# Statistics moved to ScalarE, weight loads to GpSimd's queue, and a rounding remainder made by TensorE

## Chip, cores and metric

The kernel runs on one core of a Trainium2 chip. The metric is the device time in microseconds of one execution of the whole kernel. The engines of the core are named as in the profile: PE (TensorE, with PEld for its weight loads), DVE (VectorE), ACT (ScalarE), POOL (GpSimd) and SP (SyncE, which here only issues DMAs).

## What is computed

The input x has 4 images of 16 channels and 256 x 256 pixels, in fp32. Two layers follow, each with a residual and a group normalization in front (8 groups of 2 channels).

```python
# layer 0: a convolution gives 25 logits per channel and pixel; their softmax weighs the 5x5 patch
h = gn(x)
logits = conv3x3(h, conv_w) + conv_b            # N, 16*25, H, W
weights = softmax(logits.reshape(N, C, 25, H, W), axis=2)
x = x + einsum('ncuij,ncuij->ncij', unfold5x5(h), weights)
# layer 1: a 3x3 convolution over silu(h) and over 8 cubic B-splines of h
h = gn(x)
x = x + conv(silu(h), base_w) + conv(bspline(h), spl_w) + bias
```

## The kernel before

**Stages.** The *prologue* (lines 394 to 575) loads x in eight tiles (image and half of the rows; line 413), takes group statistics with VectorE's bn_stats (lines 524 and 526; group_stats, line 133), writes each image's normalizing scale and bias to nrm, prepares the weights of both layers (prepare0, prepare1; the raw weights are loaded by lines 421 to 447), and bounds the logits. It also normalizes image 0. *Layer 0* (layer0, line 603) has two copies in the program, of which a flag selects one; here the one without a maximum runs. *Layer 1* (layer1, line 831) goes over 64 units of 16 rows.

**Normalization.** normalize (line 242) is a generator of small steps. For image b it fills zero borders in DRAM (lines 248 to 259), and for each group of 4 channels applies the scale and bias on ScalarE in two layouts: hsp by rows (line 317, stored to hs) and ht for transposition (line 330). Its inner part columns (line 339), 16 calls per image, has TensorE transpose four blocks into the PSUM tile tp (line 352), copies tp to tt (fp32) and to hi (fp32r, which rounds h), and takes the rest lo = tp - hi on VectorE (line 360). The three are stored to DRAM with line 292. SyncE's queue issues all of these DMAs. For image 0 the steps are pulled along by the prologue's loop over the tiles of x, with tp copied to tt by VectorE; for images 1 to 3 by layer 0 on the image before, one step of the generator per step of layer 0 (line 817), with ScalarE as copier. So 48 calls of columns lie in the first 48 strips of layer 0.

**Layer 0.** The work is cut into 64 strips: image, half of the rows (128 of them on the partitions), and 32 columns of the picture. A strip has 8 steps of 4 columns. For each column, TensorE multiplies the im2col columns am (fp32) and an (fp32r) by the weights, into one of three PSUM buffers lg of two columns each (lines 780 and 784). ScalarE takes Exp of two columns at a time to e (line 803); GpSimd multiplies e by the patch values u (line 808); VectorE sums numerators and denominators to nd (line 685). e has four buffers. am and an come from hst and hsl by SyncE's queue (lines 633 and 643). What follows a strip is put on a list with due steps (after and step, lines 673 to 681): seed (ScalarE, Ln and Exp, lines 698 and 699), divide (VectorE, lines 703 to 705), apply (GpSimd, line 711, which subtracts the quotient from the tile xc of x), and, once four strips have filled an xc of 128 columns, statistics (VectorE's bn_stats, line 719) and store (ScalarE's DMA queue, line 729). statistics feeds the second group normalization: scales (line 171) turns st1 into the factors of layer 1, for images 0 and 1 during the last image of layer 0, for 2 and 3 during layer 1.

**Order.** in_order (line 577) makes every engine keep the program's order in layer 0 and in layer 1; the marks of lines 821 and 823 allow SyncE and ScalarE to begin layer 1's work beside the last strips of layer 0, but the first Silu of layer 1 stays behind ScalarE's last instruction of layer 0 (line 1041). In the prologue the order within an engine isn't fixed by hand.

**Layer 1.** Per unit ScalarE makes the distances and powers (lines 931, 161 to 164) and Silu (line 913), VectorE the splines (lines 156 and 165 to 167), TensorE the products (lines 977 to 993).

```python
            def sums():
                nd, j, e, done = waiting.pop(0)
                nc.vector.tensor_reduce(
                    nd[:, :, j : j + JG, :], e.rearrange("p t j m c d -> p t j c m d"),
                    AX.XY, ALU.add,
                )
```

Of the kernel before, what the change touches and what calls it, by code (L numbers as in the profile page):

```python
# [14 lines left out]
ALU = mybir.AluOpType  # L15
# [18 lines left out]
def conv_preact_kernel(  # L34
# [95 lines left out]
    stat1 = ctx.enter_context(tc.tile_pool(name="stat1", bufs=1))  # L130
    st1 = [const.tile([P, G, NH * (W // CX), 6], F32, name=f"st1_{b}") for b in range(B)]

# [38 lines left out]
    def scales(b, psum):  # L171


        def small(n, name):
            return stat1.tile([P, n], F32, name=f"{name}_{b}", tag=f"{name}{b % 2}")

        mv = stat1.tile([P, G, 2], F32, name=f"mv_{b}", tag=f"mv{b % 2}")
        for g in range(G):
            nc.vector.bn_aggr(mv[:, g, :], st1[b][:, g].rearrange("p n s -> p (n s)"))
        yield  # L180
        ps = psum()[:, 0:G]
        nc.tensor.matmul(ps, lhsT=ones, rhs=mv[:, :, 0], start=True, stop=True)
        yield
        mean, d, rstd = small(G, "mean"), small(G, "d"), small(G, "rstd")
        q = stat1.tile([P, 6], F32, name=f"q_{b}", tag=f"q{b}")
        nc.vector.tensor_sub(d, mv[:, :, 0], ps)
        nc.vector.tensor_mul(mean, gsel_sb, ps)
        nc.vector.reduce_sum(q[:, 1:2], mean, AX.X)
        yield
        nc.scalar.activation(d, d, AF.Square)  # L190
        yield
        ps = psum()[:, 0:G]
        nc.tensor.matmul(ps, lhsT=ones, rhs=d, start=True, stop=False)
        nc.tensor.matmul(ps, lhsT=ones, rhs=mv[:, :, 1], start=False, stop=True)
        yield
        nc.vector.tensor_scalar(rstd, ps, EPS, None, ALU.add)  # L196
        yield
        nc.gpsimd.tensor_tensor(rstd, rstd, mhalf, ALU.pow)  # L198
        nc.gpsimd.tensor_mul(rstd, rstd, gsel_sb)
        yield  # L200
        nc.vector.reduce_sum(q[:, 0:1], rstd, AX.X)
        nc.vector.tensor_scalar(q[:, 1:2], q[:, 1:2], q[:, 0:1], -1.0, ALU.mult, ALU.mult)
        for k in range(2):
            nc.vector.tensor_scalar(q[:, 2 + k : 3 + k], q[:, k : k + 1], 2.5, None, ALU.mult)
        yield
        ps = psum()[:, 0:2]
        nc.tensor.matmul(
            ps, lhsT=sel.rearrange("p c s -> p (c s)"), rhs=q[0:C, 2:4], start=True, stop=True
        )
        yield  # L210
        nc.vector.tensor_copy(q[:, 4:5], ps[:, 0:1])
        nc.vector.tensor_add(q[:, 5:6], ps[:, 1:2], ub)
        sc[b] = tuple(q[:, k : k + 1] for k in (0, 1, 4, 5))
        yield
# [3 lines left out]

    nrm = [const.tile([P, 2, G], F32, name=f"nrm{b}") for b in range(B)]
    NIM = 3  # L220

    def norm_tiles(prep):
# [6 lines left out]
        ]  # L229
        for t in (*tts, *xps):  # L230
            nc.gpsimd.memset(t, 0.0)
        for t in (*his, *los):
            nc.gpsimd.memset(t.bitcast(F32), 0.0)
        return prep, xps, tts, his, los
# [6 lines left out]

    def normalize(b, ptr, tiles, held=None, copier=None):

        prep, xps, tts, his, los = tiles
        copier = copier or nc.scalar.copy
        for e in (0, HP - PAD):
            for r in range(PAD):
                nc.sync.dma_start(  # L250
                    hs[b][:, e + r].rearrange("s c w -> c s w"),
                    zero[0:C, 0 : NST * SP].rearrange("c (s w) -> c s w", s=NST),
                )
        for h in range(NH):
            for w in (0, (W + 1) * RP):
                nc.sync.dma_start(hst[b][h][:, w : w + RP], zero[0:C, 0:RP])
                nc.sync.dma_start(
                    hsl[b][h][:, :, w : w + RP].rearrange("c t r -> (c t) r"), zero[:, 0:RP]
                )
# [79 lines left out]
        def columns(q, n, h):  # L339
# [11 lines left out]
            for k in range(QG):  # L351
                nc.tensor.transpose(
                    tp[:, k, :], hts[q, h][:, n * QG + k].rearrange("p w c -> p (w c)"), ident
                )
            yield
            copy(tts[n], copier)
            copy(his[n], nc.scalar.copy)
            yield

            nc.vector.tensor_sub(  # L360
                los[n][:, h, :, 1 : 1 + P], tp, his[n][:, h, :, 1 : 1 + P].bitcast(F32)
            )
            if h == NH - 1:
                moves.append((5, partial(border, los[n])))
                moves.append((9, partial(put_columns, q, n)))
            yield
            yield
# [26 lines left out]
    with tc.tile_pool(name="prep0", bufs=2) as prep, tc.tile_pool(  # L394
# [42 lines left out]
        for d in range(3):  # L437
            dc = slice(d * C, (d + 1) * C)
            for k in range(9):
                nc.sync.dma_start(sw[:, d, k], spl_w[dc, k])  # L440
            v = spl_s[dc]
            nc.sync.dma_start(
                ss[:, d],
                bass.AP(tensor=v.tensor, offset=v.offset, ap=[v.ap[0], [0, NS], [1, 9 * nm]]),
            )
        bw = pre.tile([nm, 9, nm], F32, name="bw")
        nc.sync.dma_start(bw, base_w)

# [67 lines left out]
        for b in range(B):  # L516
# [27 lines left out]
            nc.vector.tensor_copy(nrm[b][:, 0], rstd)  # L544
            nc.vector.scalar_tensor_tensor(nrm[b][:, 1], mean, -1.0, rstd, ALU.mult, ALU.mult)
            ms = stat.tile([P, 2], F32, name=f"ms_{b}", tag="ms")
            nc.vector.tensor_mul(mean, mean, mean)
# [11 lines left out]
            if b == 0:  # L559
                ahead = normalize(0, ptr0, tiles, held, nc.vector.tensor_copy)  # L560
                next(ahead)
# [41 lines left out]
    def layer0(shift):  # L603
# [4 lines left out]
        with tc.tile_pool(name=f"prep{arm}", bufs=2) as prep, tc.tile_pool(  # L608
# [7 lines left out]
            for t in ans:  # L616
                v = t.bitcast(F32)
                nc.vector.memset(v, 0.0)
                for r in (4 * C, 6 * C):
                    nc.vector.memset(v[r : r + 1], 1.0)  # L620
            tiles = norm_tiles(prep)
# [80 lines left out]
            def divide(n, nd, xc, r):  # L702
                nc.vector.tensor_mul(nd[:, 0], nd[:, 0], r)  # L703
                nc.vector.scalar_tensor_tensor(r, nd[:, 0], 2.0, r, ALU.subtract, ALU.mult)  # L704
                nc.vector.tensor_mul(nd[:, 1], nd[:, 1], r)  # L705
                after(LAG + 3, apply, n, nd, xc)

            def apply(n, nd, xc):
                w0 = strips[n][2] * SW % CX
                v = xc[:, :, w0 : w0 + SW]  # L710
                nc.gpsimd.tensor_sub(v, v, nd[:, 1].rearrange("p j c -> p c j"))  # L711
                if w0 + SW == CX:
                    after(2, statistics, n, xc)

            def statistics(n, xc):
                b, hf, s = strips[n]
                k = hf * (W // CX) + s * SW // CX
                for g in range(G):
                    nc.vector.bn_stats(  # L719
                        st1[b][:, g, k, :],  # L720
                        xc[:, g * GC : (g + 1) * GC, :].rearrange("p c w -> p (c w)"),
                    )
                after(2, store, n, xc)

# [106 lines left out]
    def layer1(arm, last, marks):  # L831
# [3 lines left out]
        with ExitStack() as pools:  # L835
# [135 lines left out]
            def outputs(n, sx):  # L971
# [29 lines left out]
            more = chain(*(  # L1001
                scales(b, lambda: pstat.tile([P, 8], F32, name=f"ps{arm}", tag="ps"))
                for b in range(2, B)
# [92 lines left out]
```

## Time and profile before

| what | value |
|---|---|
| median of three timed runs | 3113.82 us (3112.22 to 3114.83) |
| the profiled execution | 3113.9 us |
| its span in the profile | 3112.0 us, 40438 instructions |
| busy over the span | DVE 3010.4 us, PE 2845.3, ACT 2083.5, POOL 1938.2, PEld 1494.9 |
| granted TensorE clock | 0.965 of full speed, mean |
| prologue, layer 0, layer 1 | to about 144 us, to 2110 us, to the end |

A row of the stretches gives, for each engine, the busy time and the number of instructions in the stretch, then the granted TensorE clock, the mean busy share of the 16 DMA engines and what they moved. A row of the groups gives line, engine, operation, output and inputs, shapes and count, then busy time in us, the mean duration of one in ns, and the idle time of the engine just before, with what ended it. A row of the chain or of the timeline begins with its start and duration in us. SPq is the issue of DMAs by SyncE. The duration of one instruction is some hundredths of a microsecond longer than the distance to the next one's start, since neighbours overlap; sums over a stage are made from starts.

### The profile page before, as it was taken

What the parts mean: (1) busy time and instruction counts of PE and PEld (TensorE: products, weight loads), DVE (VectorE), ACT (ScalarE), POOL (GpSimd) and SP (SyncE); (2) the same over time, 40 slices, a digit from 0 to 9 for tenths busy, and PEclk for the clock granted to TensorE, in tenths of its full rate; (3) what the DMA queues carried; (4) which work ended last, traced back from release to release, by engine and by line L of the source; (5) the groups of instructions that cost most, each with busy time, mean ns of one, the idle gap of its engine ahead of it and who ended that gap; (6) DMA issues with size and microseconds to landing.
All of it is one profiled execution on the core that took longest, in us unless ns stands there. A gap on an engine that the chain in (4) does not pass through costs nothing.

```text
span 3112.0 us, 40438 instructions
## 1 busy us (share of the span) xinstructions
PE 2845.3 (91%) x14776; PEld 1494.9 (48%) x14776; DVE 3010.4 (97%) x1733; ACT 2083.5 (67%) x2107; POOL 1938.2 (62%) x659
## 2 busy tenths in 40 slices
PE   3489999999999999999899999976999999999999
PEld 2356656656565566566565665641232223222222
DVE  6689999999999999999999999999999999999997
ACT  6466655456564465555444444458999999999996
POOL 2289999999999999999999999990000001000000
PEclk7699999999999999999999999998999999999999
DMA  7978878778877778788676666659999889999994
GB/s 222 309 206 232 241 207 224 194 212 223 239 218 214 204 198 234 215 223 231 186 192 168 167 177 180 166 135 199 193 196 195 197 193 192 194 196 197 193 197 92
DMA packets 356530, 626.34 MB, mean 201 GB/s; under 512 B 45298, under 2 KB 222692, under 8 KB 340452
## 3 DMA queue, kind: packets, MB, share of 16 engines
q1 hardware_dynamic: 323300, 606.88, 78.0%
q10 hardware_dynamic: 33024, 16.78, 1.9%
q8 instruction: 121, 1.98, 0.3%
q14 instruction: 85, 0.70, 0.1%
HBM read 513.95 MB, written 104.24 MB: 199 GB/s over the span
## 4 chain that ended last, share of the span: by engine, by line
DVE 69%; PE 11%; ACT 6%; issue 6%; DMA 5%; SPq 2%; POOL 0%; DVEq 0%; ACTq 0%; POOLq 0%
DVE nd L685 48%; PE lg L780 5%; PE yp L977 4%; DVE ta L166 3%; DVE ta L165 3%; DVE tb L166 3%; DVE tb L165 3%; DVE ring L167 2%; DMA xin<-in_x_dram 2%; PE lg L784 1%; DVE st L719 1%; DVE tb L156 1%; DVE r L704 1%; DMA sx<-x1s 1%; DVE nd L703 1%
## 5 line engine op out<-in xcount | busy, mean ns | idle before, releaser
L780 PE MATMUL lg<-wm,am 128*128 128x400 f32 x4096 | 1750.2, 508 | 122.5 <-ACT e L803 108.2
L808 POOL TENSOR_TENSOR e<-e,u 128x1600 f32<-128x1600 f32 x512 | 1788.8, 3536 | 69.4 <-ACT e L803 68.2
L685 DVE TENSOR_REDUCE nd<-e 128x128 f32<-128x3200 f32 x512 | 1747.5, 3476 | 23.3 <-POOL e L808 23.2
L803 ACT ACTIVATE e<-lg 128x800 f32<-128x800 f32 x1024 | 815.8, 836 | 896.6 <-DVE nd L685 762.7
L784 PE MATMUL lg<-wn,an 97*128 97x400 f32 x2048 | 1359.3, 664 | 0.1
L780 PEld LDWEIGHTS lg<-wm,am 128*128 128x128 f32 x4096 | 766.7, 194 | 449.4 <-ACT e L803 159.2
L977 PE MATMUL yp<-ring,wt 128*32 128x512 f32 x6144 | 737.9, 594 | 53.8 <-POOL ring L948 35.5
L784 PEld LDWEIGHTS lg<-wn,an 97*128 97x128 f32 x2048 | 391.1, 191 | 311.9 <-issue 15.7
L977 PEld LDWEIGHTS yp<-ring,wt 128*32 128x32 f32 x6144 | 210.9, 108 | 571.1 <-issue 454.0
L894 POOL MEMSET sx<- 16x256 f32 x8 | 2.4, 302 | 718.5 <-PE yp L985 278.6
L993 PE MATMUL yp<-sl,ws 64*32 64x512 f32 x1536 | 176.5, 588 | 0.0
L167 DVE SCALAR_TENSOR_TENSOR ring<-ta,ta 128x2048 f32<-128x2048 f32 (+1 forms) x64 | 147.9, 2310 | 2.5
L167 DVE SCALAR_TENSOR_TENSOR ring<-tb,tb 128x2048 f32<-128x2048 f32 x64 | 145.7, 2276 | 2.6
L166 DVE TENSOR_TENSOR ta<-ta,ta 128x2048 f32<-128x2048 f32 (+1 forms) x64 | 147.3, 2301 | 0.1
L166 DVE TENSOR_TENSOR tb<-tb,tb 128x2048 f32<-128x2048 f32 x64 | 145.3, 2271 | 0.0
L913 ACT ACTIVATE sl<-sx,q 64x2048 f32<-64x2048 f32 x64 | 133.5, 2085 | 0.3 <-DMA sx<-x1s 0.3
L164 ACT ACTIVATE ta<-ta 128x2048 f32<-128x2048 f32 (+1 forms) x64 | 123.2, 1925 | 2.0
L164 ACT ACTIVATE tb<-tb 128x2048 f32<-128x2048 f32 x64 | 120.5, 1883 | 0.8 <-POOL sx L894 0.6
L711 POOL TENSOR_TENSOR xc<-xc,nd 128x512 f32<-128x512 f32 x64 | 98.8, 1544 | 11.9 <-DVE nd L705 11.9
L198 POOL TENSOR_TENSOR rstd<-rstd,mhalf 128x8 f32<-128x8 f32 x4 | 7.5, 1866 | 158.0 <-DVE rstd L196 158.0
L993 PEld LDWEIGHTS yp<-sl,ws 64*32 64x32 f32 x1536 | 48.8, 106 | 116.2 <-issue 115.9
L931 ACT ACTIVATE xta<-xta,q 128x4096 f32<-128x4096 f32 (+4 forms) x23 | 83.7, 3640 | 0.0
(171 smaller groups left out, 1917.2 us busy)
## 6 DMA issues: line engine op xcount, KB each, us to landing
am<-hst SPq DMA_DIRECT2D x512, 194.6 KB
u<-hs SPq DMA_DIRECT2D x320, 288.0 KB
an<-hsl SPq DMA_DIRECT2D x512, 129.8 KB
xta<-x1s SPq DMA_DIRECT2D x40, 1024.0 KB
xtb<-x1s SPq DMA_DIRECT2D x40, 1024.0 KB
xtc<-x1s SPq DMA_DIRECT2D x40, 1024.0 KB
am<-hst SPq DMA_DIRECT2D x256, 129.8 KB
sx<-x1s SPq DMA_DIRECT2D x248, 128.0 KB
```

What stands on the lines that cost most here:

```text
L164: nc.scalar.activation(s1, r1, AF.Square, scale=2.0)
L165: nc.vector.scalar_tensor_tensor(s2, t, 2.0, s2, ALU.subtract, ALU.mult)
L166: nc.vector.tensor_mul(s1, s1, r1)
L167: nc.vector.scalar_tensor_tensor(f, s2, 0.0, s1, ALU.min, ALU.subtract if given else ALU.add)
L685: nc.vector.tensor_reduce(nd[:, :, j : j + JG, :], e.rearrange("p t j m c d -> p t j c m d"), AX.XY, ALU.add,)
L780: nc.tensor.matmul(lg[:, i, :NL], lhsT=am[:, o : o + P], rhs=wm.rearrange("p m c d -> p (m c d)"), start=True, stop=False,)
L784: nc.tensor.matmul(lg[:, i, :NL], lhsT=an[:, o : o + P], rhs=wn.rearrange("p m c d -> p (m c d)"), start=False, stop=True,)
L803: nc.scalar.activation(ev, lg[:, :, :NL], AF.Exp)
L808: nc.gpsimd.tensor_tensor(e[:, 1].rearrange("p j m c d -> p j (m c) d"), e[:, 0].rearrange("p j m c d -> p j (m c) d"), uv, ALU.mult,)
L913: nc.scalar.activation(sl[n % 2][:, :, 1 : W + 1], t, AF.Silu, scale=sc[b][0][0 : RD * C], bias=sc[b][1][0 : RD * C],)
L977: nc.tensor.matmul(yp[t * M : (t + 1) * M], lhsT=wt[:, d, e].rearrange("p r o -> p (r o)"), rhs=ring[:, r0 + t * RT + d : r0 + t * RT + d ...
L993: nc.tensor.matmul(yp[t * M : (t + 1) * M], lhsT=ws[:, e].rearrange("p r o -> p (r o)"), rhs=sl[n % 2][:, t : t + NT + 1 : NT, e : e + W], ...
```

## The change

Six edits, all in the functions printed above.

1. **statistics** runs on ScalarE: for each of the 8 groups of a finished xc, two activations (Identity and Square, with the first normalization's scale and bias) over 128 x 256 elements, each with its sum taken by the accumulator's output. One group per step. st1 holds these sums, and store is due two steps after apply. scales works from the sums: one reduction instead of eight aggregations, one TensorE product instead of two, more of the small operations on GpSimd.
2. **columns** for images 1 to 3: ScalarE copies the transposed layout ht, rounded, to hr; after tt and hi are copied, TensorE writes h - rounded h to tp as a sum of two products, ht with the identity (fp32) and hr with its negative (fp32r), and ScalarE copies that to lo. For image 0 VectorE's subtraction stays.
3. **divide** writes the quotient to a tile o of its own in the order channel, column; apply reads o straight.
4. The **loads of layer 1's weights** and the zero fills of image 0 are issued by GpSimd.
5. The **memsets** of the buffers xp, tt, hi, lo and an cover only borders, or the rows not filled by DMAs.
6. The prologue makes nrz, two small tiles per image, for scales.

```diff
-            nc.vector.tensor_sub(
-                los[n][:, h, :, 1 : 1 + P], tp, his[n][:, h, :, 1 : 1 + P].bitcast(F32)
-            )
+            if rest:
+                for k in range(QG):
+                    for i, (v, of) in enumerate(
+                        ((hts[q, h][:, n * QG + k], ident), (hr[:, k], nident))
+                    ):
+                        nc.tensor.matmul(
+                            tp[:, k, :], lhsT=v.rearrange("p w c -> p (w c)"), rhs=of,
+                            start=i == 0, stop=i == 1,
+                        )
+                yield
+                nc.scalar.copy(los[n][:, h, :, 1 : 1 + P], tp)
+            else:
+                nc.vector.tensor_sub(
+                    los[n][:, h, :, 1 : 1 + P], tp, his[n][:, h, :, 1 : 1 + P].bitcast(F32)
+                )
+                yield
...
+            if rest:
+                hr = prep.tile([P, QG, W // QW, QC], F32R, name=f"hr{b}_{q}_{n}_{h}", tag="hr", bufs=1)
+                nc.scalar.copy(hr, hts[q, h][:, n * QG : (n + 1) * QG])
...
-                nc.sync.dma_start(sw[:, d, k], spl_w[dc, k])
+                nc.gpsimd.dma_start(sw[:, d, k], spl_w[dc, k])
...
-                ahead = normalize(0, ptr0, tiles, held, nc.vector.tensor_copy)
+                ahead = normalize(0, ptr0, tiles, held, nc.vector.tensor_copy, nc.gpsimd)
...
-                v = t.bitcast(F32)
-                nc.vector.memset(v, 0.0)
-                for r in (4 * C, 6 * C):
-                    nc.vector.memset(v[r : r + 1], 1.0)
+
+                nc.vector.memset(t.bitcast(F32)[4 * C : KT], 1.0)
...
-                nc.vector.tensor_mul(nd[:, 1], nd[:, 1], r)
-                after(LAG + 3, apply, n, nd, xc)
-
-            def apply(n, nd, xc):
+
+                o = ndp.tile([P, C, SW], F32, name=f"o_{n}{arm}", tag="o", bufs=1)
+                nc.vector.tensor_mul(o.rearrange("p c j -> p j c"), nd[:, 1], r)
+                after(LAG + 3, apply, n, o, xc)
+
+            def apply(n, o, xc):
                 w0 = strips[n][2] * SW % CX
                 v = xc[:, :, w0 : w0 + SW]
-                nc.gpsimd.tensor_sub(v, v, nd[:, 1].rearrange("p j c -> p c j"))
+                nc.gpsimd.tensor_sub(v, v, o)
                 if w0 + SW == CX:
-                    after(2, statistics, n, xc)
-
-            def statistics(n, xc):
+                    for g in range(G):
+                        after(1 + g, statistics, n, xc, g)
+                    after(2, store, n, xc)
+
+            def statistics(n, xc, g):
                 b, hf, s = strips[n]
                 k = hf * (W // CX) + s * SW // CX
-                for g in range(G):
-                    nc.vector.bn_stats(
-                        st1[b][:, g, k, :],
-                        xc[:, g * GC : (g + 1) * GC, :].rearrange("p c w -> p (c w)"),
+                z = l0.tile([P, GC * CX], F32, name=f"z_{n}_{g}{arm}", tag="z", bufs=1)
+                v = xc[:, g * GC : (g + 1) * GC, :].rearrange("p c w -> p (c w)")
+                for t, f in enumerate((AF.Identity, AF.Square)):
+                    nc.scalar.activation(
+                        z, v, f, scale=nrm[b][:, 0, g : g + 1], bias=nrm[b][:, 1, g : g + 1],
+                        accum_out=st1[b][:, t, g, k : k + 1],
                     )
-                after(2, store, n, xc)
...
-        mv = stat1.tile([P, G, 2], F32, name=f"mv_{b}", tag=f"mv{b % 2}")
-        for g in range(G):
-            nc.vector.bn_aggr(mv[:, g, :], st1[b][:, g].rearrange("p n s -> p (n s)"))
+        sums, d, mz, p = small(2 * G, "sums"), small(G, "d"), small(G, "mz"), small(G, "p")
+        q = stat1.tile([P, 6], F32, name=f"q_{b}", tag=f"q{b}")
+        nc.vector.tensor_reduce(sums, st1[b].rearrange("p t g k -> p (t g) k"), AX.X, ALU.add)
```

## Prediction

> **What bounds the kernel now.** I read the page first, then the engines' busy time by stretch. The work has three stages: a prologue (statistics of x, first normalization) up to about 144 us, layer 0 up to 2110, layer 1 up to the end.
>
> ```profile
> core 0: us, PE busy (x) PEld busy (x) DVE busy (x) ACT busy (x) POOL busy (x), PEclk, DMA share, GB/s
> 640.00:1125.00 485.00, 457.99 (x1600) 295.69 (x1600) 483.90 (x224) 271.02 (x415) 468.62 (x145) 0.98 0.79 217
> ...
> 2110.00:3100.00 990.00, 959.26 (x8165) 270.54 (x8169) 976.28 (x554) 950.59 (x446) 25.49 (x34) 0.99 0.90 190
> ```
>
> In layer 0 VectorE works 483.9 of 485 us, GpSimd 468.6: VectorE sets the pace and GpSimd is only 3% behind. ScalarE has 214 us free. Layer 1 is full on VectorE and nearly so on ScalarE, and the change hardly touches it. The chain of work that ended last shows what VectorE's time in a strip of layer 0 consists of:
>
> ```profile
> 543.96 0.07 DVE nd L705
> 544.03 0.54 issue
> 544.57 0.68 DVE lo L360
> 545.25 27.14 DVE nd L685 x8
> 572.40 2.62 DVE st L719 x8
> ...
> 577.05 27.15 DVE nd L685 x8
> ...
> 606.25 27.15 DVE nd L685 x8
> ...
> 635.45 27.15 DVE nd L685 x8
> ```
>
> The bare strip lasts 29.20 us (577.05 to 606.25 to 635.45): eight sums and the three products of the division. L719 adds 2.62 in one strip of four, L360 0.60 in each of the first 48. VectorE in layer 0: 64 x 29.20 + 48 x 0.60 + 15 x 2.62 = 1936.9 us (the sixteenth L719 falls at the border to layer 1). Layer 0 lasts 1965 us, from GpSimd's first product at 144.4 to its last subtraction at 2109.7; filling, draining and a 13 us stall at 150 are the rest. The groups by shape, for the other engines:
>
> ```profile
> L808 POOL TENSOR_TENSOR e<-e,u 128x1600 f32<-128x1600 f32 x512 | 1788.8, 3536 | 69.4 <-ACT e L803 68.2 <-DMA u<-hs 1.0
> L711 POOL TENSOR_TENSOR xc<-xc,nd 128x512 f32<-128x512 f32 x64 | 98.8, 1544 | 11.9 <-DVE nd L705 11.9
> L330 ACT ACTIVATE ht<-xp,nrm 128x512 f32<-128x512 f32 x48 | 63.5, 1323 | 0.0
> L705 DVE TENSOR_TENSOR nd<-nd,r 128x512 f32<-128x512 f32 x64 | 43.9, 686 | 2.2
> L491 DVE TENSOR_REDUCE wc<-sw 128x48 f32<-128x432 f32 x3 | 2.4, 857 | 0.0
> ```
>
> GpSimd's products follow each other every 3.49 us (six in 20.93), so a strip costs it 8 x 3.49 + 1.48 = 29.4. TensorE is closer than its busy share says. In a stretch where it never waits:
>
> ```profile
> 1266.84 0.84 PE L780 MATMUL lg<-wm,am 128*128 128x400 f32 x2
> 1267.18 0.19 PEld L784 LDWEIGHTS lg<-wn,an 97*128 97x128 f32 x1
> ...
> 1267.51 0.55 PEld L352 LDWEIGHTS tp<-ident,ht 128*128 128x128 f32 x4
> 1267.70 0.60 PE L352 MATMUL tp<-ident,ht 128*128 128x128 f32 x4
> 1268.03 0.30 PEld L780 LDWEIGHTS lg<-wm,am 128*128 128x128 f32 x2
> 1268.14 0.84 PE L780 MATMUL lg<-wm,am 128*128 128x400 f32 x2
> ```
>
> A column of logits takes 0.858 us from start to start, a strip of 32 of them 27.4, and four transposes about 0.44 (1.30 from one L780 to the next, less 0.858): 27.9 us, 2.5 below VectorE. So little room is left: whatever VectorE loses beyond one us per strip, another engine takes over.
>
> **The parts of the change.**
>
> *Statistics to ScalarE.* VectorE loses 15 x 2.62 = 39.3 us in layer 0. ScalarE gains 256 activations of 128x256. Its rows: a 128x512 copy 591 ns, a 128x8 copy 196, so 0.39 us for 256 elements; L317, with pointers for scale and bias, stands 0.2 above that line: 0.6 us. The accumulator's output has no row; between nothing and 0.2 more. Per strip 4 x 0.6 to 0.8 = 2.4 to 3.2 us, beside about 17 busy of 30.3: hidden. They come two per step of 3.7 us, so the Exp that GpSimd waits for is late by at most 1.6, and four buffers of e cover that.
>
> *The rounding's rest on TensorE.* VectorE loses 48 x 0.60 = 28.8 us. ScalarE gains two copies of 0.6 in each of 48 calls: hidden. TensorE gains per call four fp32 products (two records each) and four fp32r ones, 128 columns wide: 12 records. The nearest row is the transpose, one record of that shape in 0.11: 1.3 us. Bounds: 1.1 if only streaming counts (at L780's 0.34 per 400 columns a record is 0.107, and fp32r half of that), 1.8 if fp32r this narrow runs like fp32. I take 1.3, as every record brings a weight load of its own, like the transposes. TensorE's strip becomes 27.9 + 1.3 = 29.2, level with VectorE. The new products also wait for ScalarE's copies of tp, and all later logits queue behind them; three buffers of lg hold a step and a half of work meanwhile.
>
> *The quotient in channel order.* L705 now writes o with 128 B from element to element, and GpSimd reads it straight. GpSimd: 512 elements at 3.49/1600 per element are 1.1 instead of 1.48, so its strip falls to 29.0. For the write, the trace shows no strided one on VectorE. From below it costs nothing (0.69 stays; no reason for a gain). From above: L330 writes with 512 B steps on ScalarE, 1.18 apart, where contiguous L317 with 64 elements more needs 0.79: 0.44 more. L491 reads on VectorE with 192 B steps: 0.81 apart for 432 elements, where L685's rate gives 0.52; scaled to 512, 0.34 more. [...] I take 29.54, VectorE's own row.
>
> So VectorE remains just the bound: 64 x 29.54 = 1890.6, against 1936.9: **46.3 us less**. The scales of two batches, inside the last batch, lose eight aggregations (1.1 us) and a little each: 2.4 less. Their added GpSimd work, 1.5 us each, lies under its slack.
>
> *Weights and zeros on GpSimd's queue.* SyncE's queue in the prologue:
>
> ```profile
> 35.55 5.70 SPq L440 DMA_DIRECT2D sw<-in_spl_w_dram  x9
> ...
> 62.07 1.01 SPq L278 DMA_DIRECT2D hs<-hsp  x2
> 63.17 1.32 SPq L413 DMA_DIRECT2D xin<-in_x_dram  x1
> ```
>
> From 35.55 to 62.07 it issues 31 weight loads and 12 zero fills, and behind them the sixth tile of x, though its buffer is free at 32 (last L526 on it) and the hs<-hsp ahead of it are ready at 39; the DMA engines are only 0.16 to 0.35 busy there. That tile's landing starts the rest of the prologue. Moved away, it can be issued at about 43. But ScalarE is busy without a gap from 31 to 61.6 and has its work for this tile behind that, so of 20 us about 12 are gained. GpSimd then issues 43 DMAs ahead of and between the pow operations (L152, the first due at 29.0). SyncE needs 0.64 each; no row shows one from GpSimd. [...] I take half of that: **9 us less**, between 5 more and 20 less. The smaller memsets are in the DMA-bound start of layer 0 (share 0.99): nothing.
>
> *The border to layer 1.* The last strip's 16 activations (8 to 10 us) stand on ScalarE before the first Silu; 5.7 of that is time in which it waits for x1s now. The store follows four of them: Silu some 2 to 4 us later, with VectorE behind ScalarE there. Against that stand L719's last 2.6 us and the cheaper scales of layer 1. Zero, from 5 less to 4 more.
>
> Sum: 3113.9 (the profiled execution; its span is 3112.0, the median of the timed runs 3113.8) - 46.3 - 2.4 - 9 = **3056**.
>
> **Rivals.** (1) *TensorE becomes the bound in the first 48 strips*: fp32r like fp32 (1.8) and 0.4 of waiting per call, 30.1 per strip. 48 x 30.1 + 16 x 29.54 = 1917.4, 19.5 saved, with the 11.4 beside: 3083. For it: 27.9 already. Against: nothing shows fp32r slow; in the chain of waits L784's 400 columns take 0.19, half of one L780 record (0.34). (2) *The strided write is free* and three engines share the bound at about 29.45 (29.2 in the last batch): 1880.8, 56.1 saved, and 15 in the prologue: 3040. (3) *Slower: TensorE waits for ScalarE in each call.* If its lead is gone when it reaches the new products, it stands for an Exp (0.84) and four copies (1.6) each time: 29.2 + 2.4 = 31.6 per strip, 48 of them and 16 x 29.54 are 1989, 52 more than VectorE has now: 3155. It decides from 1.7 us per call on. Against: ScalarE has a third of its time free, and a waiting TensorE still leaves a step of logits in PSUM. (4) *The cover eats everything*: rival 1 with the prologue lost, about no change.
>
> **Chances.** Main case 0.50, (1) 0.22, (2) 0.20, (4) 0.03, (3) 0.05. About 0.2% is what a measurement can tell from no change. Faster 0.92, same 0.03, slower 0.05. The range runs from 3034, under (2) with a still better prologue, to 3088, over (1).
>
> **What would show it.** L705 at about 1.0 us (right) or 0.69; L711 at 1.15; the bare strip 29.5 with VectorE over 99% busy in 640 to 1125; TensorE over 97% there would speak for (1), waits of the tp products for ScalarE for (3). The sixth tile's load near 43, layer 0 starting near 135. Wrong if layer 0 shrinks by less than 30 us, or if the prologue grows.

## The result and the profile after

| | before | after |
|---|---|---|
| median, four runs each | 3113.02 us (3111.94 to 3114.83) | 3093.6 us (3088.9 to 3097.72) |
| ratio, 95% interval | | 0.9937, 0.9919 to 0.9954 |
| profiled execution, span | 3113.9, 3112.0 | 3088.9, 3087.0 |
| start to GpSimd's first product | 144.4 | 130.6 |
| layer 0 (to the end of the last apply) | 1965.3 | 1942.3 |
| from there to the end | 1002.3 | 1014.1 |

The kernel became faster, by 19.4 us in the medians where 57.7 were forecast. The profiled execution, the quickest of the four, is 25.0 shorter: 13.8 in the prologue (9 forecast) and 23.0 in layer 0 (48.7; under 30 was the forecast's sign of being wrong), less 11.8 given back at the border (0). These stages are of one execution each. The runs z_outside, last_left_out and sync_queue below do the same work in layer 0, and in the four it took 1938.7 to 1954.6 us: a difference of a few microseconds in one stage can be scatter. The rows by stretch of the changed kernel:

```profile
core 0: us, PE busy (x) PEld busy (x) DVE busy (x) ACT busy (x) POOL busy (x), PEclk, DMA share, GB/s
640.00:1125.00 485.00, 476.44 (x1806) 318.19 (x1806) 475.60 (x178) 334.25 (x580) 469.70 (x146) 1.00 0.83 218
2110.00:3100.00 990.00, 949.44 (x8092) 263.25 (x8084) 951.06 (x521) 932.26 (x437) 34.81 (x31) 1.00 0.88 185
```

VectorE fell from 483.90 to 475.60 of 485, TensorE rose from 457.99 to 476.44: three engines are within 7 us of each other. TensorE at 98% is the sign that the forecast named for its rival 1. (The second stretch isn't the same work in both kernels: layer 1 starts 37 us earlier here.) In the chain that ended last, VectorE's sums carried a bare strip of before, and VectorE 69% of the whole span, TensorE 11%. Now it is 39% and 35%, and for long stretches the chain runs along TensorE's logits, with the new products among them:

```profile
519.50 0.68 PE lg L810 x2
520.17 0.19 PE lg L814
520.36 1.29 PE tp L378 x12
521.65 0.72 PE lg L810 x2
...
656.24 1.37 PE tp L378 x12
```

The twelve records (single MATMULs of the trace) that one call of columns adds take 1.29 to 1.37 us (1.3 forecast). The groups by shape, first two rows of before, then those of after:

```profile
L685 DVE TENSOR_REDUCE nd<-e 128x128 f32<-128x3200 f32 x512 | 1747.5, 3476 | 23.3 <-POOL e L808 23.2
...
L803 ACT ACTIVATE e<-lg 128x800 f32<-128x800 f32 x1024 | 815.8, 836 | 896.6 <-DVE nd L685 762.7 <-PE lg L784 121.7 <-DVE q L201 3.7
```

```profile
L838 POOL TENSOR_TENSOR e<-e,u 128x1600 f32<-128x1600 f32 x512 | 1789.9, 3535 | 63.4 <-ACT e L833 53.9 <-DMA u<-hs 5.8 <-ACT ht L340 3.1
L710 DVE TENSOR_REDUCE nd<-e 128x128 f32<-128x3200 f32 x512 | 1747.8, 3478 | 53.0 <-POOL e L838 52.4
...
L833 ACT ACTIVATE e<-lg 128x800 f32<-128x800 f32 x1024 | 840.8, 840 | 664.4 <-PE lg L814 413.2 <-DVE nd L710 236.9 <-PE lg L810 3.7
...
L750 ACT ACTIVATE z<-xc,nrm 128x256 f32<-128x256 f32 x256 | 153.1, 598 | 10.6 <-POOL xc L738 6.1
L738 POOL TENSOR_TENSOR xc<-xc,o 128x512 f32<-128x512 f32 x64 | 84.3, 1318 | 13.4 <-DVE o L732 13.4
L732 DVE TENSOR_TENSOR o<-nd,r 128x512 f32<-128x512 f32 x64 | 69.5, 1085 | 2.3
...
L750 ACT ACTIVATION_READ_ACCUMULATOR z<-xc,nrm 128x1 f32 x256 | 48.7, 190 | 0.0
```

Exp now waits 413 us for TensorE's logits (122 before), and VectorE's sums 52 us for GpSimd (23 before). The strided write (L732) takes 1.085 us where L705 took 0.686; apply (L738) takes 1.32 and not 1.54 (1.15 was forecast). An activation of the statistics is two instructions, 0.60 and 0.19, one pair each 0.73.

The distance from one apply to the next gives the length of a strip, as GpSimd sees it. For the 16 strips of image 1 (positions 0 to 15 in what follows):

```
after   29.3 29.6 30.6 29.7 30.5 30.6 29.3 33.1 30.7 29.3 29.3 29.1 29.1 29.1 29.1 32.6
```

Images 0 to 2 took 484.6, 486.7, 488.8 before, and 482.3, 481.0, 477.1 after; 16 x 29.54 = 472.6 were forecast. The last image (15 distances) went from 423.1 to 418.1, 5.0 less; the forecast's own terms give 5.2 (three L719 and the scales, less 15 x 0.34). So the sum held in the image without calls of columns, and failed in the three with them.

### The profile page after: what moved, and what is told of

Same layout as the page of the kernel before. It is cut to its first block, busy times and chain, and to the rows that moved or that the text cites. A ratio compares the mean times of both kernels' runs of the same rounds, so it can differ in the third digit from the quotient of the medians.

```text
span 3087.0 us, 41924 instructions
## 1 busy us (share of the span) xinstructions
PE 2884.5 (93%) x15336; PEld 1545.9 (50%) x15336; DVE 2951.5 (96%) x1524; ACT 2297.7 (74%) x2715; POOL 1951.8 (63%) x734
## 4 chain that ended last, share of the span: by engine, by line
DVE 39%; PE 35%; ACT 9%; issue 6%; DMA 4%; POOL 3%; SPq 2%; DVEq 0%; ACTq 0%; POOLq 0%
PE lg L810 22%; DVE nd L710 22%; PE lg L814 6%; PE yp L1007 4%; DVE ta L169 3%; DVE tb L169 3%; DVE tb L168 3%; DVE ta L168 3%; POOL e L838 2%; DVE ring L170 2%; PE tp L378 2%; DMA an<-hsl 1%; DVE tb L159 1%; ACT ta L167 1%; ACT ta L164 1%
## 5 line engine op out<-in xcount | busy, mean ns | idle before, releaser
L810 PE MATMUL lg<-wm,am 128*128 128x400 f32 x4096 | 1729.4, 503 | 60.7 <-ACT e L833 34.3
L814 PE MATMUL lg<-wn,an 97*128 97x400 f32 x2048 | 1343.7, 656 | 5.3 <-DMA an<-hsl 5.3
L833 ACT ACTIVATE e<-lg 128x800 f32<-128x800 f32 x1024 | 840.8, 840 | 664.4 <-PE lg L814 413.2
L810 PEld LDWEIGHTS lg<-wm,am 128*128 128x128 f32 x4096 | 761.3, 192 | 359.3 <-ACT e L833 55.1
L750 ACT ACTIVATE z<-xc,nrm 128x256 f32<-128x256 f32 x256 | 153.1, 598 | 10.6 <-POOL xc L738 6.1
L169 DVE TENSOR_TENSOR ta<-ta,ta 128x2048 f32<-128x2048 f32 (+1 forms) x64 | 148.4, 2318 | 2.1 <-ACT ta L167 2.1
L170 DVE SCALAR_TENSOR_TENSOR ring<-tb,tb 128x2048 f32<-128x2048 f32 x64 | 145.6, 2276 | 2.6
L169 DVE TENSOR_TENSOR tb<-tb,tb 128x2048 f32<-128x2048 f32 x64 | 145.2, 2268 | 0.7 <-ACT tb L167 0.7
L738 POOL TENSOR_TENSOR xc<-xc,o 128x512 f32<-128x512 f32 x64 | 84.3, 1318 | 13.4 <-DVE o L732 13.4
```

The source lines that it names most:

```text
L169: nc.vector.tensor_mul(s1, s1, r1)
L170: nc.vector.scalar_tensor_tensor(f, s2, 0.0, s1, ALU.min, ALU.subtract if given else ALU.add)
L750: nc.scalar.activation(z, v, f, scale=nrm[b][:, 0, g : g + 1], bias=nrm[b][:, 1, g : g + 1], accum_out=st1[b][:, t, g, k : k + 1],)
L810: nc.tensor.matmul(lg[:, i, :NL], lhsT=am[:, o : o + P], rhs=wm.rearrange("p m c d -> p (m c d)"), start=True, stop=False,)
L814: nc.tensor.matmul(lg[:, i, :NL], lhsT=an[:, o : o + P], rhs=wn.rearrange("p m c d -> p (m c d)"), start=False, stop=True,)
L833: nc.scalar.activation(ev, lg[:, :, :NL], AF.Exp)
```

## Experiments

Theory: (a) a call takes six steps of the generator and a strip has eight, so calls are 1.33 per strip in twelve strips of an image (1 to 12 of 0 to 15, by their place in the trace) and none in the other four; with one call TensorE needs 27.44 + 0.44 + 1.31 = 29.2 us, with two 30.9. TensorE is the bound there. (b) The 11.8 us at the border are the last strip's activations and the memory of their output z. Rivals: the strided write on VectorE; no gain in the prologue; DMA. Times beside which no other is given are to be held against 3093.6 after; stages are of the profiled execution.

**The prologue: weights and zeros back on SyncE.**

```diff
-                nc.gpsimd.dma_start(sw[:, d, k], spl_w[dc, k])
+                nc.sync.dma_start(sw[:, d, k], spl_w[dc, k])
```
(and ss, bw and the zero fills likewise)

> The weight loads and the zero fills of image 0 go back to SyncE's queue, all else as changed. Theory (the queue made the prologue's gain): GpSimd's first product at 142 to 145 us instead of 130.6, the time rises by 11 to 14 us to about 3105. Rival (the shorter memsets made it): first product stays within 3 us of 130.6.

3109.19 us (ratio 0.9984, 0.9978 to 0.9991); GpSimd's first product at 145.6 (144.4 before). The whole gain of the prologue is this move. All other runs below keep it, and their first product stands at 131.5 to 133.8, so the 13.8 of the one execution is at the upper end. In the changed kernel, SyncE's queue shows the sixth tile of x, then the seventh; in this run the sixth is issued at 63.19:

```profile
42.38 1.02 SPq L288 DMA_DIRECT2D hs<-hsp  x2
43.50 1.34 SPq L438 DMA_DIRECT2D xin<-in_x_dram  x1
...
63.79 0.88 SPq L438 DMA_DIRECT2D xin<-in_x_dram  x1
```

**The products left out.** lo gets a copy of tp, which still holds h.

```diff
-                for k in range(QG):
-                    for i, (v, of) in enumerate(
...
                 yield
                 nc.scalar.copy(los[n][:, h, :, 1 : 1 + P], tp)
```

> Leaves out the eight products of the rounding's rest per call of columns (lo then holds a copy of h itself); all copies stay. Theory (TensorE is the bound in the twelve strips of an image that have calls, at 27.4 + 1.33 x 1.75 = 29.8): these fall to VectorE's 29.5 or a little below, and TensorE can make good its waits for DMAs: an image takes 472 to 475 us instead of 477 to 482, the time falls by 12 to 20 us. Rival (VectorE stays the bound and ScalarE's longer queue makes the losses): an image stays at 477 to 482, the time within 4 us of 3093.

3070.39 us (0.9857, 0.984 to 0.9873), 23.2 less in the medians. Images 0 to 2 took 474.0, 477.4, 472.4: 16.6 us less than after, of the 22.5 above 3 x 472.6 (the profiled execution is the slowest of its four here, and the quickest for after). Strips fell to 29.1 between applies, but those at positions 7 and 15 stayed at 31.7 to 35.5 (29.2 at the end of image 2), and one other took 33.5.

These distances are GpSimd's, and VectorE's own are another matter. At position 7 of image 0 GpSimd waited 1.85 us for late logits while VectorE summed on without a gap, 29.47 us from one division to the next:

```profile
436.23 3.55 POOL L830 TENSOR_TENSOR e<-e,u 128x1600 f32<-128x1600 f32 x1 [1.85 <-ACT e L825]
```

```profile
431.74 1.06 DVE L724 TENSOR_TENSOR o<-nd,r 128x512 f32<-128x512 f32 x1
432.64 27.22 DVE L702 TENSOR_REDUCE nd<-e 128x128 f32<-128x3200 f32 x8
...
461.21 1.08 DVE L724 TENSOR_TENSOR o<-nd,r 128x512 f32<-128x512 f32 x1
```

So VectorE, at 29.5, is still the slowest of the engines where nothing holds TensorE up: GpSimd, at 29.1, runs ahead of it into the buffers of e, and a late transfer costs time only as far as VectorE itself comes to wait. What VectorE waited between 200 and 1610 (us, times, longest), after and without the products:

```profile
DVE nd L710 <- POOL e L838: 23.2, 24, 2.0
```

```profile
DVE nd L702 <- POOL e L830: 9.5, 8, 2.0
```

**The remainder back on VectorE, for all images.**

```diff
-        rest, copier = copier is None, copier or nc.scalar.copy
+        rest, copier = False, copier or nc.scalar.copy
```

> VectorE makes the rounding's remainder for images 1 to 3 too, as before the change; everything else as after it. Theory (a call of columns is 1.33 per strip in the first 12 strips of an image, none in the last 4): VectorE then needs 29.54 + 1.33 x 0.60 = 30.34 us in each of the 12 and 29.54 in the other 4, 482 us per image, and TensorE falls to about 28.0 and has slack again, so that the store's DMA holes are hidden. Images 0 to 2 measured 482.1, 481.1 and 477.1 with the remainder on TensorE: layer 0 should grow by only 0 to 8 us, the time be 3092 to 3102. Rival (the remainder's products are pure loss on TensorE and taking them away is what counts, whoever takes the work): layer 0 shrinks as without products, by 15 or more, to 3075.

3095.06 us (0.9942, 0.9925 to 0.9958), images 484.7, 484.1, 477.3, TensorE 457.34 of 485 in 640 to 1125, as before the change (457.99). VectorE hardly waits between 200 and 1610:

```profile
DVE nd L710 <- POOL e L838: 3.8, 5, 1.2
```

The move from VectorE to TensorE bought 1.5 us of median, within the scatter: 0.60 per call taken from one bound, 1.31 given to the next.

**The straight write.** nd keeps the quotient, apply reads across it.

```diff
-                o = ndp.tile([P, C, SW], F32, name=f"o_{n}{arm}", tag="o", bufs=1)
-                nc.vector.tensor_mul(o.rearrange("p c j -> p j c"), nd[:, 1], r)
+                nc.vector.tensor_mul(nd[:, 1], nd[:, 1], r)
```

> The quotient stays in nd in the order column, channel: VectorE's last product of the division writes straight again, and GpSimd's apply reads across. Theory (TensorE sets the pace of the first 12 strips of images 0 to 2): VectorE gives up 0.40 us per strip and GpSimd takes some 0.25 more, and neither is the bound there: images 0 to 2 stay within 2 us of 482, 481 and 477, only the last image (VectorE the bound) shortens by 2 to 6. Time 3086 to 3092. Rival (VectorE still sets the pace and the strided write is what the forecast lost): 64 x 0.40 = 25 us less, 3068.

3101.59 us (0.9958, 0.9942 to 0.9975), 8 us longer: both missed, the rival by 34. VectorE's write fell back to 0.69, and its idle time behind GpSimd between 200 and 1610 grew from 23.2 to 39.5 us. Undisturbed strips take 29.3 to 29.4 between applies, not 29.1: after any wait it is GpSimd that catches up (29.4 per strip straight, 29.1 with o), and at 29.4 it gains nothing on a VectorE that needs 29.2 (the bare strip of before). The strided write costs VectorE 0.40 a strip. That it is worth this rests on these waits and on 8 us between medians whose ranges touch (3096.12 to 3104.58, after 3088.9 to 3097.72).

**Calls of seven steps** (1.14 per strip).

```diff
                 moves.append((8, partial(put_columns, q, n)))
+            if rest:
+                yield
```

> One more empty step per call of columns, so that the 16 calls of an image spread over nearly 15 strips instead of 12; nothing else changes. Theory (TensorE the bound where the calls crowd): a strip has 1.14 calls and costs TensorE 29.4, level with VectorE; an image takes 474 to 478 us instead of 477 to 482, the time falls by 8 to 14 us to about 3082. Rival (VectorE the bound all along): no change, 3090 to 3096.

3092.08 us (0.9932, 0.9916 to 0.9949): mostly missed. Four or five strips of each image still take 30.2 to 31.9 and most others 29.3 to 29.5, and the work pushed back meets the end of images 0 and 1 (35.1, 32.6).

**One record in place of two.** The fp32 product of the sum is made in the transposing mode.

```diff
-                            start=i == 0, stop=i == 1,
+                            start=i == 0, stop=i == 1, is_transpose=i == 0,
```

> In columns, the first of the two products of each sum (ht with the identity in fp32, two records) is made in the transposing mode (one record); the second, hr with the negative identity, is added to it as before. A call then adds 8 records of 128 columns to TensorE and not 12. Theory (TensorE is the bound where calls fall, at 0.11 us per record): a call costs 0.44 us less, strips with two calls fall from 30.6 to about 30.1, those with one stay at 29.3; layer 0 is 5 to 12 us shorter, 3079 to 3088. Rival (not the records count but the products and their waits for ScalarE's copies): no change within 3 us of 3091.

3082.24 us (0.9905, 0.9888 to 0.9921); strips 29.1, with 29.5 in some of those that had 30.6. The eight records of a call take 0.76 us, from the first one's start to the next logits, where the twelve took 1.29. That is 0.095 us per record and 0.11: the cost goes with the number of records.

**The remainder added in place.** z lasting (below), and hr with the negative identity is added to what stands in tp; of the four transposes only the first has start set.

```diff
-                nc.tensor.transpose(
-                    tp[:, k, :], hts[q, h][:, n * QG + k].rearrange("p w c -> p (w c)"), ident
+                nc.tensor.matmul(
+                    tp[:, k, :], lhsT=hts[q, h][:, n * QG + k].rearrange("p w c -> p (w c)"),
+                    rhs=ident, start=k == 0 or not rest, stop=True, skip_group_check=rest, is_transpose=True,
...
-                    for i, (v, of) in enumerate(
-                        ((hts[q, h][:, n * QG + k], ident), (hr[:, k], nident))
-                    ):
-                        nc.tensor.matmul(
+                    nc.tensor.matmul(
+                        tp[:, k, :], lhsT=hr[:, k].rearrange("p w c -> p (w c)"), rhs=nident,
+                        start=False, stop=True, skip_group_check=True,
...
```

> As z_outside, and the rounding's remainder is made by adding hr with the negative identity to the transposed block that already stands in tp: four products per call, the four in fp32 are gone. Theory: a strip of TensorE is 27.44 + 1.33 x (0.44 + 0.5) = 28.7 us, below GpSimd's 29.1 and VectorE's 29.5, so layer 0 is as short as without any products (16 to 20 less than after the change), and layer 1 as with z lasting (7 less): 3063 to 3073. Rival (TensorE's wait for the copies of tp is the loss, and it stays): 3080 to 3086.

3064.41 us (0.9846, 0.9829 to 0.9862), layer 0 1923.5 (1925.1 without products), from its end on 1006.6. The four records take 0.40, 0.10 each. Four products per call are as good as none.

**Half and half.** Straight write, seven steps, z lasting, and TensorE's remainder only for every second call (`if rest and n == 0`).

> As z_outside and seven_steps and straight_order together, and only every second call's remainder is made by TensorE, the other by VectorE. Theory: per strip VectorE 29.2 + 0.57 x 0.60 = 29.5, TensorE 27.44 + 1.14 x 0.44 + 0.57 x 1.3 = 28.7, GpSimd 29.4: GpSimd and VectorE share the bound, TensorE has a lead again; images 0 to 2 take 473 to 477 each (482, 481, 477 after the change), layer 1 1006: 3068 to 3078. Rival (GpSimd at 29.4 catches up too slowly after each hole, as in straight_order): 3085 to 3095.

3065.56 us (0.9845, 0.9829 to 0.9862), a little better than expected; images 475.6, 477.9, 472.4.

**z lasting.**

```diff
+    zt = const.tile([P, GC * CX], F32, name="zt")
...
-                z = l0.tile([P, GC * CX], F32, name=f"z_{n}_{g}{arm}", tag="z", bufs=1)
...
-                        z, v, f, scale=nrm[b][:, 0, g : g + 1], bias=nrm[b][:, 1, g : g + 1],
+                        zt, v, f, scale=nrm[b][:, 0, g : g + 1], bias=nrm[b][:, 1, g : g + 1],
```

> The scratch tile z of the statistics is a lasting tile, so no memory of layer 1 has to wait for it. Theory (the border lost 12 us because layer 1's tiles lie where z lay: VectorE's L170 waits 9.3 us, GpSimd's L1040 11.5, the xtb load till after the last z): the first half of layer 1's first unit runs beside the statistics, layer 1 from the last apply to the end takes 1005 to 1007 us instead of 1014, the time falls by 7 to 10 us to about 3084. Rival (the 16 activations cost by standing in ScalarE's queue, wherever z lies): no change, 3090 to 3096.

3088.86 us (0.9915, 0.9898 to 0.9931), 4.7 less where 7 to 10 were expected, but from the last apply to the end it took 1006.7, as expected. (Layer 0 of this execution was a long one, 1954.6.)

**The last strip's statistics left out**, with z lasting; a GpSimd memset puts 1.0 in their place.

```diff
-                    for g in range(G):
+                    for g in range(G if n + 1 < len(strips) else 0):
```

> As z_outside (z is one lasting tile), and of the last strip the 16 activations of the statistics are left out (a constant is put in their place, so the second normalization of image 3 is not the reference's). Theory (the growth of layer 1 is those activations ahead of the first Silu, and the use of z's memory): from the last apply to the end 1000 to 1004 us, against 1014 after and 1006.6 with z lasting; time 3079 to 3087. Rival (the rest of the growth comes from elsewhere, such as the longer sums of scales in layer 1): layer 1 stays at 1006 to 1007.

3078.22 us (0.9889, 0.9872 to 0.9905), from the last apply to the end 999.8. The border's 11.8 us are these activations: 7.4 go with the memory of z (1014.1 to 1006.7), 6.9 with their place ahead of layer 1's work on ScalarE (1006.7 to 999.8), and what then remains is 2.5 shorter than before (1002.3). This stage hardly scatters: it takes 1013.3 to 1015.4 in all runs with z as changed, and 1005.9 to 1008.4 in all with z lasting and the activations in place. In the changed kernel, ScalarE and then VectorE at the border:

```profile
2072.93 0.60 ACT L750 ACTIVATE z<-xc,nrm 128x256 f32<-128x256 f32 x1 [6.11 <-POOL xc L738]
...
2084.32 0.19 ACT L750 ACTIVATION_READ_ACCUMULATOR z<-xc,nrm 128x1 f32 x1
2084.53 1.91 ACT L164 ACTIVATE tb<-xta 128x2048 f32<-128x2048 f32 x1
```

```profile
2071.71 3.60 DVE L169 TENSOR_TENSOR ta<-ta,ta 128x2304 f32<-128x2304 f32 x1
2084.59 2.56 DVE L170 SCALAR_TENSOR_TENSOR ring<-ta,ta 128x2304 f32<-128x2304 f32 x1 [9.28 <-ACT z L750]
...
2100.67 1.23 DVE L159 TENSOR_SCALAR tb<-xtb 128x2048 f32<-128x2048 f32 x1 [5.71 <-ACT xtb L961]
```

VectorE's next row of the splines, which has nothing to do with the statistics, stands 9.28 us until the last z is written, and again 5.71 for xtb, whose load was held up likewise. Without the activations, VectorE runs through:

```profile
2069.25 3.61 DVE L170 TENSOR_TENSOR ta<-ta,ta 128x2304 f32<-128x2304 f32 x1
2072.95 2.56 DVE L171 SCALAR_TENSOR_TENSOR ring<-ta,ta 128x2304 f32<-128x2304 f32 x1
```

**The long strips.** At positions 7 and 15 TensorE waits for am or an; these are the holes of what follows. In the changed kernel, SyncE's queue and then TensorE at such a place (the store of an xc was issued on ScalarE's queue at 666.0):

```profile
659.10 13.25 SPq L682 DMA_DIRECT2D u<-hs  x5
...
675.94 4.66 SPq L658 DMA_DIRECT2D am<-hst  x3
```

```profile
683.39 1.20 PE L810 MATMUL lg<-wm,am 128*128 128x400 f32 x2 [3.25 <-DMA am<-hst]
684.58 0.67 PE L814 MATMUL lg<-wn,an 97*128 97x400 f32 x1
685.05 1.53 PE L810 MATMUL lg<-wm,am 128*128 128x400 f32 x2
```

Five issues that otherwise take 2.27 us stand for 13.25 behind the store. TensorE waits 3.25 and then runs slow: a pair of L810 takes 1.20 and 1.53 in place of 0.84, at a granted clock of 0.59 between 684 and 688.

First idea: the store comes too early, two steps after apply.

```diff
-                    after(2, store, n, xc)
+                    after(4, store, n, xc)
```

> The store of a finished xc is due four steps after apply, as before the change, and not two. Theory (the earlier store falls together with the load of the next strip's u on SyncE's queue, am comes late, and TensorE, without slack, waits): the strips of 33 to 35 us at positions 7 and 15 of images 0 to 2 fall to about 31, which is 6 to 15 us: 3079 to 3088. Rival (any store in a layer without slack makes the same hole, wherever it is put): within 4 us of 3091, the holes only move.

3109.14 us (0.9988, 0.9979 to 0.9997): the theory fell, and so did the rival. The strips at 7 grew to 35.6 to 36.6: now the queue stands with the load of am itself at its head (one group of three issues took 16.26 us). Second idea: it is the size, so in four parts, two steps apart, on top of added_in_place.

```diff
-                    after(2, store, n, xc)
+                    for k in range(4):
+                        after(2 + 2 * k, store, n, xc, slice(4 * k, 4 * k + 4))
...
```

> As added_in_place, and the store of a finished xc (1 MB) is issued in four parts of four channels, two steps apart, the first where the whole one stood. Theory (the holes are SyncE's queue standing behind the store while its bytes drain, 57 to 75 us in all on u and 34 on an, so that am comes late): with 256 KB at a time the queue stands a quarter as long each time and am's two steps of lead cover it; the strips of 32 to 36 us at positions 7 and 15 of images 0 to 2, some 21 us above 29.1 in added_in_place, lose half of that: 3050 to 3058. Rival (it is the amount of bytes in these strips, however they are issued): within 3 us of 3064.

3086.53 us (0.991, 0.9893 to 0.9926), 22 longer than added_in_place: wrong again. With seven steps beside it:

> As store_in_parts, and a call of columns takes seven steps and not six, as in seven_steps. Theory (what is left at position 7 is the burst of the second group's stores and loads of the normalization, which seven steps spread out, while the image's end keeps its flush): 2 to 8 below store_in_parts, 3046 to 3056. Rival (TensorE has a lead again, so the spreading of calls is worth nothing): within 2 us of store_in_parts.

3083.86 us (0.9898, 0.9882 to 0.9915), 2.7 lower, within the scatter; 34.3, 35.7 and 35.9 at position 8. What SyncE's queue waited for between 200 and 1610, the rows of x1s, for the changed kernel and with four parts:

```profile
SPq L682 <- DMA x1s<-xc: 75.1, 8, 11.1
...
SPq L668 <- DMA x1s<-xc: 34.2, 3, 11.7
```

```profile
SPq L657 <- DMA x1s<-xc: 74.3, 15, 10.9
SPq L681 <- DMA x1s<-xc: 54.4, 8, 7.9
...
SPq L667 <- DMA x1s<-xc: 44.0, 11, 5.3
```

(In us, times, longest.) 109 us in 11 waits became 173 in these 34 (two further lines add 21 in six): each store holds the queue, a quarter of the bytes for half as long (5.1 us per wait, where it was 9.9). Third idea: it is where the store is issued. On top of added_in_place:

```diff
-                nc.scalar.dma_start(v[hf * P : (hf + 1) * P, :, c0 : c0 + CX], xc)
+                nc.gpsimd.dma_start(v[hf * P : (hf + 1) * P, :, c0 : c0 + CX], xc)
```

> As added_in_place, with the store of a finished xc issued by GpSimd and not by ScalarE, at the same step. Theory (SyncE's queue stands behind a store issued on ScalarE's hardware queue, about 5 us per issue at 256 KB and 10 at 1 MB, and not for the bytes on the DMA engines): SyncE's waits for x1s, 110 us between 200 and 1610, mostly go, the holes at positions 7 and 15 shrink to 31 or less; GpSimd gives some 0.6 us per store for its issue: 3046 to 3057. Rival (the bytes hold the queue whoever issues them): SyncE's waits stay at 80 us or more and the time at 3062 to 3070.

3058.11 us (0.9823, 0.9806 to 0.9839), the quickest version here. No wait for x1s is left in SyncE's queue, and none of TensorE for am or an; the queue's first rows:

```profile
SPq L657 <- PE lg L812: 516.9, 167, 6.1
SPq L667 <- PE lg L812: 25.0, 57, 0.9
```

Images 0 to 2 took 470.6, 470.7, 471.9, without a strip above 30.4, and VectorE never waited between 200 and 1610; the issue costs GpSimd 1.2 us (30.3 against 29.1) in one strip of four. Last, seven steps on top of added_in_place, with the store on ScalarE:

> As added_in_place, and a call of columns takes seven steps and not six. Theory (TensorE has a lead again, so evenness of the calls is worth nothing, but the burst of DMAs at the half of an image is spread, as in seven_steps): the hole at position 7 goes, the image's end keeps its own: 3056 to 3063. Rival (the hole only moves to another strip): 3063 to 3070.

3063.22 us (0.9844, 0.9828 to 0.9861), in its layer 0 1920.7 against 1923.5: the hole at 7 went, those at the image's end stayed, and the medians can't be told apart.

## Why the prediction fell short, step by step

**Failed: "TensorE's strip becomes 27.9 + 1.3 = 29.2, level with VectorE".** The price of a call was right (1.29 to 1.37), and so is the mean of one call per strip; but the calls don't lie one to a strip. The generator's yields say six steps per call, and a strip has eight. In the trace of the changed kernel the twelve strips of an image with calls have 1, 2, 1, 1, 2, 1, 1, 2, 1, 1, 2, 1 sets of the new products, and never two sets of transposes beside two of products. A strip with two sets needs 27.44 + 0.44 + 2 x 1.31 = 30.5 us of TensorE (not 30.9, as theory (a) has it), a microsecond more than VectorE; measured are 30.6 (29.3 with one). The four strips without calls give nothing back, since VectorE takes its 29.5 there all the same. Twelve such strips in three images are some 13 us. Without the products VectorE waited 13.7 less (23.2 to 9.5) and the images took 16.6 less.

This is rival 1 in its place, with another reason: fp32r was not slow (a call took 1.29 to 1.37 us, not that rival's 1.8) and the waits were small (TensorE waited 5.4 us for Exp between 200 and 1610, against 70 before). That rival 1 puts layer 0 at 21.9 less (19.5 and the scales), so near the measured 23.0, is luck.

**Failed by omission: no room for DMA.** The stretch without a wait that I read showed TensorE's lead, not what it was for. Before, SyncE's queue stood 92 us for the same stores between 200 and 1610, and TensorE did not feel it: its waits there name Exp and lo only. After the change they name am and an. The queue's waits before, then TensorE's before and after:

```profile
SPq L633 <- DMA x1s<-xc: 39.2, 5, 8.4
SPq L292 <- DMA x1s<-xc: 30.7, 3, 10.6
SPq L643 <- DMA x1s<-xc: 21.7, 3, 7.3
```

```profile
PE lg L780 <- ACT e L803: 70.1, 36, 4.2
PE tp L352 <- DVE lo L360: 6.5, 3, 2.2
```

```profile
PE lg L810 <- DMA am<-hst: 12.0, 7, 3.2
PE lg L810 <- ACT e L833: 5.4, 6, 1.3
PE lg L814 <- DMA an<-hsl: 4.1, 11, 0.6
```

With the remainder back on VectorE, TensorE again has some 2 us a strip in hand; it stood 24.7 us for am and an there, and of that little reached VectorE (3.8). So the lead is what takes late transfers up. It doesn't explain all of it: before, TensorE had no such waits at all, though the queue stood 92 us for the stores (119 in that run). VectorE's 2.62 us of bn_stats in every fourth strip, gone with the change, may have given the loads their time; no run tests this.

The rest of the 22.5 us above 3 x 472.6, some 6 to 9, are such holes; with the products cut to four and the store on GpSimd's queue, images 0 to 2 take 1413.2 us in all, and the forecast's 3 x 472.6 = 1417.9 is reached.

**Failed: the border, "Zero, from 5 less to 4 more"; it was 11.8 more.** I counted the activations before Silu only. They also stand before the powers of layer 1 (L164), and z was a new reader and writer of memory that layer 1 takes over, so VectorE and the next load waited for the last of them. For that memory, 7.4 us, the forecast had no term.

**Right: the strided write**, 29.54 for VectorE's strip: measured from one division to the next 29.5. By the row of L705 alone it would have been 29.20; by VectorE's own strided read, L491, it is 0.34 more. That L491's loss lies in its steps and carries over to a write was the author's estimate; the write of L732 costs 0.40 (1.085 against 0.686). "VectorE remains just the bound" holds for the strips without a second set of products and without a hole: in store_by_gpsimd, where both are gone, it never waits between 200 and 1610. In the changed kernel VectorE's sums carry 36% of the chain between 200 and 2040, and TensorE's logits 45% (78% and 9% before). GpSimd, at 29.1 (29.0 forecast), runs ahead of VectorE.

**Right in direction: the prologue**, -13.8 for -9 (-10.6 to -12.9 in the other runs with the move): the sixth tile was issued at 43.50 (43 forecast). Of about 12 I had docked 3, as half of a delay of pow by slow issues on GpSimd. No run shows that term: GpSimd's DMAs here take 0.49 to 0.56 us each, where SyncE's weight loads before took 0.63. The first pow starts at 32.2 (29.0 before), and the last thing it waits for is VectorE's variance (1.77 us), not an issue.

**Right: ScalarE's cover** in the strips (0.73 per activation, 0.6 to 0.8 forecast), the scales as far as the last image shows them, and that rival 3 does not occur.

Together: -13.8 - 23.0 + 11.8 = -25.0 in the profiled execution, against -57.7. The 32.7 between are 22.5 in images 0 to 2 (13 to 17 of products, the rest holes), 11.8 at the border and 3.2 of layer 0 that no run assigns (the last apply alone took 1.9 longer), less 4.8 more in the prologue. How products and holes share the 22.5 is rough, since the holes differ from execution to execution.

The version with the products cut, z lasting and the store moved is another kernel, but it shows what the forecast's terms were worth without the three things it left out: 10.6 less in the prologue (9 forecast), 47.8 in layer 0 (48.7), 3.6 more at the border (0), and 3058.11 us for 3056.

## What to carry to other kernels

When work is moved to an engine that is close behind, count how often per period it falls there at its densest, from the program's own schedule, not its mean over the stage. An engine's lead can be what takes up late transfers; before spending it, look up what waits in the DMA queues and how long. Judge a late strip by the waits of the slowest engine, not by the rhythm of one that runs ahead of it. At the border of two stages, ask whose memory the new tile's memory becomes.

## What was not expected of the hardware

- A store issued on ScalarE's queue held SyncE's queue for some 10 us at 1 MB (109.3 in 11 waits for x1s) and 5 at 256 KB (172.7 in 34); issued by GpSimd, at the same bytes, not at all (no wait for x1s between 200 and 1610). What in the chip makes one queue stand for the other was not tried.
- A TensorE wait of 3.25 us (from 680.1) was followed by a granted clock of 0.59 for some 4 us. A shorter one did the same: 2.02 us before 443.86, and 0.51 from 444.9 to 448.3. One of 1.92 before 927.32 did not: 1.00 from 926 to 936.
- The last apply on GpSimd took 3.42 us beside VectorE's L168 and L169, of which L169 took 3.60. The 64 applies take 1.32 on average, and L166 before the change, at the same shape as this L169, took 2.55.
